# A two-layer perceiver block on one core: low halves on GpSimd, gated products in 512 columns

## The chip, the cores and the metric

The kernel runs on one core of one Trainium2 chip. A core has five engines with queues of their own: TensorE (PE) multiplies matrices into PSUM, VectorE (DVE), ScalarE (ACT) and GpSimd (POOL) do element-wise work, and SyncE (SP) here issues all the DMAs. GpSimd reads and writes only SBUF in this program; results in PSUM are read by DVE or ACT. The metric is the device time of one execution in microseconds (us), lower is better.

## The reference

There are 128 sequences of 32 tokens with 256 features, and a context of 257 tokens for each. Two layers follow each other, and each has three sublayers with a residual sum:

```python
x = x + L0_xattn(layernorm(x), ctx)      # A: 16 features a head, rms norm of q and k
x = x + L0_attn(layernorm(x))            # B: differential attention with rotary embedding
x = x + L0_ffn(layernorm(x))             # C: silu(x w1^T) * (x w2^T), 704 wide, weights rounded to NF4
x = x + L1_xattn(layernorm(x), mask, ctx) # D: 32 heads of 8; masked self-attention plus gated cross-attention
x = x + L1_attn(layernorm(x))            # E: 16 heads of 16, causal
x = x + L1_ffn(layernorm(x))             # F: router, 8 experts: w_e * ((silu(x Wg) * (x Wu)) Wd)
```

All inputs and outputs are float32.

## The kernel before

Four sequences make one block of 128 tokens, one token to a partition, so there are 32 blocks (`h`, or `u` where the context attention counts both layers). F and C take two blocks at a time (`g`, 16 of them).

**Precision.** A float32 operand of a matmul is split into a high and a low half of 16 bits, and a product is the sum of high x high, high x low and low x high. `split_ps` (lines 437 to 444) makes both halves from a PSUM bank: ACT copies the bank to float16 (high), and DVE subtracts that from the bank (low). `expP` (line 1026) does it in another way for the weights of the context attention: ACT writes the exponential as float32 (`P`), a bfloat16 view of its upper 16 bits serves as the high half, and POOL subtracts that view to make the low half (`Pl`). The hidden values of C and F (`hid`, `fhid`, with `hidl`, `fhl`) go that second way too.

**Streams and the order of work.** Each sublayer is a Python generator (`A_prep`, `rowpass`, `pvpass`, `attn_fin`, `B_gen`, `C_gen`, `D_prep`, `D_self`, `E_gen`, `E_att`, `F_gen`, `F_down`) that issues some instructions and yields. `pipeline` (line 411) holds a planner (`Est`): it has a cost for every instruction on each engine, keeps a time line of each engine, and always steps the stream whose next inputs are due first. The order it finds for each engine is pinned; the engines then wait for each other by semaphores. A change of any cost therefore rewrites the order of everything behind it. Every instruction is issued through line 290, so the profile's lines are all L290 and the names of the tiles tell the groups apart.

**PSUM** has 8 banks of 512 float32 columns. `tk` (line 386) hands out the one that the planner expects to be free first.

**The parts that the change touches:**
- `ln_raw` (533): two transposes of the block into a bank, the split into `hT`, and the statistics of the norm. B, D, E and A use it. `mm_tok` (495) multiplies `hT` by weights.
- `D_prep` (1273) makes queries, keys and values of a block for D; `D_self` (1325) does its self-attention: scores into `dS` (128 x 1024), a maximum over 32 columns for each of 32 groups (`s`), its subtraction, the exponential, then for each of two halves four transposes, the split into `dPT`, and the products with the values. The maximum is issued as follows:

```python
nc.vector.tensor_reduce(mx, Sf, AX.X, ALU.max)
nc.vector.tensor_tensor(Sf, Sf, mb, ALU.subtract)
nc.scalar.activation(Sf, Sf, AF.Exp)
```

- `E_gen` (1385) makes `qa`, `ka` and `va` of a block for E.
- `C_gen` (1231) and `F_gen` (1563): for each block of 128 hidden features, the gate and the up product of two token blocks (256 columns each) go side by side into one bank; ACT takes the tanh of the gate half (`glu_t`), DVE makes (tanh + 1) x gate and multiplies it by the up half, POOL makes the low half. C has six such blocks (the last of 64 features), F two for each of eight experts. `F_down` (1587) multiplies by the down weights, up to two experts behind.

The context work of layer 1 also prepares the keys and values that layer 2 reads back from DRAM.

Of the kernel before, what the change touches and what calls it, by code (L numbers as in the profile page):

```python
# [12 lines left out]
F32 = mybir.dt.float32  # L13
F16 = mybir.dt.float16
# [351 lines left out]
class Body:  # L366
# [70 lines left out]
    def split_ps(self, ps, hi, lo, scale=None):  # L437
# [4 lines left out]
        else:  # L442
            nc.scalar.activation(hi, ps, AF.Copy, scale=scale)
            nc.vector.scalar_tensor_tensor(lo, ps, scale, hi, ALU.mult, ALU.subtract)

    def rsqrt(self, o, a, eps):
        w, n = a.shape[0], a.shape[-1]
        if a.space != PSUM:
            self.nc.scalar.activation(o, a, AF.Copy, bias=eps)
        else:  # L450
            self.nc.vector.tensor_scalar(o, a, eps, None, ALU.add)
        self.nc.gpsimd.tensor_tensor(o, o, self.nhalf[:w, :n], ALU.pow)
# [42 lines left out]
    def mm_tok(self, ps, hT, tt, W, c0, N):  # L495
        nc = self.nc
        seq = [(a, b, k) for a, b in ((0, 0), (0, 1), (1, 0)) for k in (0, 1)]
        for i, (a, b, k) in enumerate(seq):
            nc.tensor.matmul(ps, hT[:, a, k, tt * 128:tt * 128 + 128], W[b][:, k, c0:c0 + N], start=(i == 0), stop=(i == len(seq) - 1))

# [6 lines left out]
    def ln_T(self, xts, pool, tag=None):  # L507
        nc = self.nc
        n = len(xts)
        mv = self.sm.tile([128, 2, 2], F32, name="bmv")  # L510
        for t in range(n):
            st = self.sm.tile([128, 6], F32, name="bst")
            nc.vector.bn_stats(st, xts[t])
            nc.vector.bn_aggr(mv[:, t, :], st)
        rs = self.sm.tile([128, 2], F32, name="brs")
        self.rsqrt(rs[:, :n], mv[:, :n, 1], 1e-5)
        hs = []
        nm = self.sm.tile([128, 2], F32, name="bnm")
        for t in range(n):
            nc.gpsimd.tensor_scalar(nm[:, t:t + 1], mv[:, t, 0:1], rs[:, t:t + 1], -1.0, ALU.mult, ALU.mult)  # L520
            h = pool.tile([128, 256], F32, name=f"lnh{t}", tag=tag, bufs=tag and n)
            nc.scalar.activation(h, xts[t], AF.Identity, bias=nm[:, t:t + 1], scale=rs[:, t:t + 1])
            hs.append(h)
        yield "end"
        ps = self.tk()
        for t, h in enumerate(hs):
            for k in range(2):
                nc.tensor.transpose(ps[:, (k * n + t) * 128:(k * n + t) * 128 + 128], h[:, k * 128:k * 128 + 128], self.ident)
        hT = pool.tile([128, 2, 2, 128 * n], F16, name="hT")
        self.split_ps(ps[:, :256 * n], hT[:, 0].rearrange("p k t -> p (k t)"), hT[:, 1].rearrange("p k t -> p (k t)"))  # L530
        return hT

    def ln_raw(self, xt, pool):
        nc = self.nc
        ps = self.tk()
        for k in range(2):
            nc.tensor.transpose(ps[:, k * 128:k * 128 + 128], xt[:, k * 128:k * 128 + 128], self.ident)
        hT = pool.tile([128, 2, 2, 128], F16, name="hT")
        self.split_ps(ps[:, :256], hT[:, 0].rearrange("p k t -> p (k t)"), hT[:, 1].rearrange("p k t -> p (k t)"))
# [616 lines left out]
    def setup_C(self):  # L1156
        nc, T = self.nc, self.T
        yield from self.need(("set", "A"))
        w1T = [self.w0.tile([128, 2, 704], BF, name=f"ffn{i}") for i in range(2)]
        self.w12T = w1T  # L1160
# [4 lines left out]
        for wi in range(3):  # L1165
# [47 lines left out]
            if wi < 2:  # L1213
                for k in range(2):
                    ps = self.tk().bitcast(BF)
                    for r in range(8):
                        nc.tensor.transpose(ps[:, r * 88:r * 88 + 88], wq[:, r * 256 + k * 128:r * 256 + k * 128 + 128], self.identb[:88, :88])
                    nc.vector.tensor_copy(w1T[wi][:, k, :].rearrange("p (s r) -> p r s", r=8), ps[:, :704].rearrange("p (r s) -> p r s", r=8))
                    yield "end"
            else:  # L1220
# [3 lines left out]
                for ft in range(6):  # L1224
# [4 lines left out]
                    yield "end"  # L1229

    def C_gen(self, g):
        nc = self.nc
# [5 lines left out]
        hl = self.cw.tile([128, 6, 256], F16, name="hidl")  # L1238
        for ft in range(6):
            n = FT[ft]  # L1240
            ps = self.tk()
            for u in range(2):
                seq = [(k, a) for k in (0, 1) for a in (0, 1)]
                for i, (k, a) in enumerate(seq):
                    nc.tensor.matmul(ps[:n, u * 256:u * 256 + 256], self.w12T[u][:, k, ft * 128:ft * 128 + n], hT[:, a, k, :], start=(i == 0), stop=(i == 3))
            t = self.cw.tile([128, 256], F32, name="glu_t", bufs=2)
            nc.scalar.activation(t[:n], ps[:n, :256], AF.Tanh, scale=0.5)
            nc.vector.scalar_tensor_tensor(t[:n], t[:n], 1.0, ps[:n, :256], ALU.add, ALU.mult)
            nc.vector.tensor_tensor(hid[:n, ft], t[:n], ps[:n, 256:512], ALU.mult)
            nc.gpsimd.tensor_tensor(hl[:n, ft], hid[:n, ft], hid[:n].bitcast(BF)[:, ft, 1::2], ALU.subtract)  # L1250
            yield "pe" if ft < 5 else [hl]
        hv = hid.bitcast(BF)
# [20 lines left out]
    def D_prep(self, h):  # L1273
# [6 lines left out]
        yield "end"  # L1280
        hT, rs = self.ln_raw(xt, self.dw)
        yield [hT, rs]
        yield from self.need(("cen",), *[("Ds", h - 1)] * (h > 0))
# [41 lines left out]
    def D_self(self, h):  # L1325
# [21 lines left out]
        nc.vector.tensor_reduce(mx, Sf, AX.X, ALU.max)  # L1347
        nc.vector.tensor_tensor(Sf, Sf, mb, ALU.subtract)
        nc.scalar.activation(Sf, Sf, AF.Exp)
# [3 lines left out]
        for q2 in range(2):  # L1353
            ps = self.tk()
            for q in range(4):
                nc.tensor.transpose(ps[:, q * 128:q * 128 + 128], S[:, q2 * 4 + q].rearrange("p b k -> p (b k)"), self.ident)
            PT = self.dw.tile([128, 2, 4, 128], F16, name="dPT")
            self.split_ps(ps, PT[:, 0].rearrange("p q t -> p (q t)"), PT[:, 1].rearrange("p q t -> p (q t)"))
            yield [PT]
            pr = self.tk()  # L1360
            for q in range(4):
                for a in range(2):
                    nc.tensor.matmul(pr[:, q * 4:q * 4 + 4], PT[:, a, q, :], self.ones4, start=(a == 0), stop=(a == 1))
            nc.vector.reciprocal(rs[:, :, q2 * 4:q2 * 4 + 4].rearrange("p b a -> p a b"), pr[:, :16].rearrange("p (a b) -> p a b", b=4))
            ps = self.tk()
            for q in range(4):
                qd = q2 * 4 + q
                for i, (a, d) in enumerate(((0, 0), (0, 1), (1, 0))):
                    nc.tensor.matmul(ps[:, q * 128:q * 128 + 128], PT[:, a, q, :], self.Vd[:, d, qd].rearrange("p b c -> p (b c)"), start=(i == 0), stop=(i == 2))
            for hh in range(4):  # L1370
# [14 lines left out]
    def E_gen(self, h):  # L1385
        nc = self.nc
        yield from self.need(("att", self.NH + h), ("set", "E"))
        xt = self.xt[self.NH + h]
        hT, rs = self.ln_raw(xt, self.ew)
        rq = self.sm.tile([128, 1], F32, name="rrq")  # L1390
        nc.scalar.activation(rq, rs, AF.Copy, scale=IWS)
        yield [hT, rq]
        ps = self.tk()
# [169 lines left out]
    def F_gen(self, g):  # L1563
# [6 lines left out]
        for e in range(8):  # L1570
            yield from self.need(*[("Fd", g * 8 + e - 2)] * (g * 8 + e > 1))
            hid = self.fw.tile([128, 2, 256], F32, name="fhid", bufs=2)
            hl = self.fw.tile([128, 2, 256], F16, name="fhl", bufs=2)
            for ft in range(2):
                ps = self.tk()
                for u, nm in enumerate((f"wg{e}", f"wu{e}")):
                    self.mm_feat(ps[:, u * 256:u * 256 + 256], self.W[nm], ft * 128, 128, lambda k: hT[:, 0, k, :], lambda k: hT[:, 1, k, :])
                t = self.fw.tile([128, 256], F32, name="glu_t", bufs=2)
                nc.scalar.activation(t, ps[:, :256], AF.Tanh, scale=0.5 * IWS)
                nc.vector.scalar_tensor_tensor(t, t, 1.0, ps[:, :256], ALU.add, ALU.mult)  # L1580
                nc.vector.tensor_tensor(hid[:, ft], t, ps[:, 256:512], ALU.mult)
                nc.gpsimd.tensor_tensor(hl[:, ft], hid[:, ft], hid.bitcast(BF)[:, ft, 1::2], ALU.subtract)
                yield "pe"
            self.fh[g * 8 + e] = (hid, hl, w)
# [192 lines left out]
```

## Time and profile before

| what | value |
|---|---|
| time, three runs | 3371.24, 3372.80, 3373.25 us; median 3372.8 |
| the profiled execution | 3372.91 us, of which the span of the instructions is 3371.1 |
| mean granted TensorE clock | 0.937 of full speed |
| context and layer 1, 300 to 1500 us: PE, DVE, ACT, POOL busy | 1153.2, 804.4, 956.3, 901.4 of 1200 us |
| passage between the layers, 1500 to 1800 us | 236.5, 207.1, 194.0, 159.3 of 300 us |
| layer 2, 1800 to 3300 us | 1361.5, 1182.7, 954.7, 914.0 of 1500 us |

The span is the time from the first to the last instruction of the program in one profiled execution. Busy time is the time in which an engine had an instruction at work; the end of a matmul is modelled, so a busy TensorE need not be TensorE at its peak. The granted clock is the share of the full clock that the throttle let TensorE have. In a row of groups, the shapes stand as out<-in (partitions x columns, type), then the count, the busy time, the mean of one instruction in ns, and the idle time of that engine just before those instructions with what ended it. "X <- Y" in a list of waits means that X stood idle until Y was done.

### The profile page before, as it was taken

The numbers are of one execution on the slowest core, as the hardware profiler recorded it, in microseconds if no ns is written. First come the engines' busy times: TensorE is split into PE (matmuls) and PEld (weight loads), VectorE is DVE, ScalarE is ACT, GpSimd is POOL, SyncE is SP. The second block draws the span as 40 slices with busy tenths as digits, with TensorE's granted clock in tenths as the row PEclk, the third lists the DMA queues.
The fourth block names the chain that finished last, engine by engine and source line by source line (L and its number), as shares of the span: only waits on it lengthen the run. The fifth ranks groups of instructions, "written<-read, shape, count | busy, mean of one in ns | idle before, by whom it ended". The sixth has DMA issues, their size and how long they took to land. (4 is left out here: it accounts for less than half of the span.)

```text
span 3371.1 us, 106946 instructions
## 1 busy us (share of the span) xinstructions
PE 3022.6 (90%) x41537; PEld 2271.9 (67%) x41537; DVE 2451.2 (73%) x6084; ACT 2246.3 (67%) x6477; POOL 2104.3 (62%) x2537
## 2 busy tenths in 40 slices
PE   3888999999999999998777999889989889989899
PEld 1455776666766666665555777667777777777677
DVE  4787666766667666666767778777888788787866
ACT  2455888878887787786666656666676666656562
POOL 1354787777777777775454756556666656656463
PEclk9899999999999999999876999889999899988889
DMA  4565777777777777776565444544454445445420
GB/s 105 156 178 156 207 220 213 223 214 209 217 222 215 220 204 206 211 219 168 142 163 135 111 107 98 126 111 113 110 133 100 121 106 123 107 98 122 107 60 14
DMA packets 687849, 511.64 MB, mean 152 GB/s; under 512 B 224396, under 2 KB 675340, under 8 KB 687340
## 3 DMA queue, kind: packets, MB, share of 16 engines
q1 hardware_dynamic: 687340, 504.80, 55.1%
q8 instruction: 326, 5.34, 0.7%
q14 instruction: 183, 1.50, 0.2%
HBM read 319.86 MB, written 180.19 MB: 148 GB/s over the span
## 5 line engine op out<-in xcount | busy, mean ns | idle before, releaser
L290 POOL TENSOR_TENSOR Pl<-P 128x512 f16<-128x512 f32 x768 | 805.9, 1064 | 241.3 <-ACT P L290 232.4
L290 DVE TENSOR_REDUCE mx<-bank 128x2 f32<-128x512 f32 x768 | 479.8, 679 | 28.2 <-PE bank L290 25.2
L290 ACT ACTIVATE P<-bank 128x512 f32<-128x512 f32 x768 | 438.6, 599 | 89.1 <-PE bank L290 63.1
L290 ACT COPY Uc<-bank 32x68 f32<-32x68 f32 x1536 | 314.7, 205 | 108.0 <-PE bank L290 88.3
L290 DVE TENSOR_TENSOR vv<-bank,vv 128x256 f16<-128x256 f32 x512 | 215.2, 424 | 145.2 <-ACT vv L290 139.7
L290 POOL TENSOR_TENSOR fhl<-fhid 128x256 f16<-128x256 f32 x256 | 156.5, 612 | 250.2 <-DVE fhid L290 238.8
L290 ACT CAST vv<-bank 128x256 f16<-128x256 f32 x512 | 203.3, 402 | 156.9 <-DVE vv L290 84.9
L290 PE MATMUL bank<-V,P 128*128 128x68 f16 (+1 forms) x4096 | 295.5, 197 | 10.4 <-DVE mx L290 3.9
L290 PE MATMUL bank<-V,Pl 128*128 128x36 f16 (+1 forms) x3072 | 280.8, 191 | 11.3 <-POOL Pl L290 9.3
L290 PEld LDWEIGHTS <-Kst 97*128 97x128 f16 x4096 | 232.8, 100 | 78.1 <-issue 51.2
L290 PEld LDWEIGHTS <-P 128*128 128x128 bf16 x4096 | 258.1, 100 | 24.5 <-issue 7.9
L290 ACT ACTIVATE glu_t<-bank 128x256 f32<-128x256 f32 x352 | 134.7, 383 | 192.3 <-PE bank L290 170.1
L290 PEld LDWEIGHTS <-Pl 128*128 128x128 f16 x3072 | 235.0, 98 | 37.0 <-POOL Pl L290 21.8
L290 DVE SCALAR_TENSOR_TENSOR glu_t<-glu_t,bank 128x256 f32<-128x256 f32 x352 | 145.1, 412 | 116.4 <-ACT glu_t L290 115.2
L290 PEld LDWEIGHTS <-ch 128*128 128x128 f16 x2048 | 191.7, 99 | 56.1 <-issue 27.2
L290 PE MATMUL bank<-QstD,Kst 97*128 97x128 f16 x2048 | 200.4, 228 | 27.8 <-DVE rbt L290 5.5
L290 PEld LDWEIGHTS <-hT 128*128 128x128 f16 x1536 | 138.5, 102 | 107.7 <-issue 30.5
L290 POOL TENSOR_TENSOR kk<-kb,kk 128x512 f16<-128x512 f32 x128 | 146.0, 1160 | 94.0 <-ACT kk L290 92.7
L290 PE MATMUL bank<-khf,eh 32*128 32x256 f16 (+1 forms) x1536 | 162.7, 284 | 46.4 <-DVE mx L290 10.2
L290 POOL TENSOR_TENSOR cl<-ct,ch 128x1024 f16<-128x1024 f32 x64 | 136.6, 2135 | 44.8 <-ACT ch L290 42.7
L290 DVE SCALAR_TENSOR_TENSOR xt<-bank,w,xt 128x256 f32<-128x256 f32 x256 | 120.0, 472 | 21.5 <-PE bank L290 20.1
L290 PEld LDWEIGHTS <-eh 32*128 32x128 f16 (+1 forms) x1536 | 53.1, 93 | 121.9 <-issue 107.9
(483 smaller groups left out, 9098.2 us busy)
## 6 DMA issues: line engine op xcount, KB each, us to landing
Kst<-kd SPq DMA_DIRECT2D x384, 256.0 KB
kd<-kk SPq DMA_DIRECT2D x128, 512.0 KB
vd<-vv SPq DMA_DIRECT2D x256, 136.0 KB
V<-vd SPq DMA_DIRECT2D x64, 544.0 KB
vd<-vv SPq DMA_DIRECT2D x256, 132.0 KB
V<-vd SPq DMA_DIRECT2D x64, 528.0 KB
ct<-in_ctxm SPq DMA_DIRECT2D x64, 512.0 KB
khf<-kd SPq DMA_DIRECT2D x128, 256.0 KB
```

Source lines behind the costliest of these rows:

```text
L290: r = f(*a, **k)
```

## The change

- `split_sb` is new. ACT copies the bank to float32 in SBUF; the upper 16 bits, read as bfloat16, are the high half, and POOL subtracts them from the copy to make the float16 low half. The blocks of D and E in `ln_raw` and the attention weights `dPT` of `D_self` use it in place of `split_ps`.
- In `D_self` the maxima are subtracted by POOL.
- C and F put two blocks of 128 hidden features into one step: two banks, one with two gate blocks and one with two up blocks, and tanh, products and low half over 512 columns (`glu`). C's weights are padded from 704 to 768 columns with zeros, so that its last block has 128 rows.
- In `E_gen` one ACT instruction with a repeated operand writes both copies of the keys' high half.
- Tiles grow to fit: `lnh` shares the tag of `glu_t` and so is allotted 512 columns. The program's dynamic DMA scratch is set to 8192.

```diff
+    def split_sb(self, ps, pool, name, tag=None, **kw):
+        nc = self.nc
+        n = ps.shape[-1]
+        f = pool.tile([128, n], F32, name=name, tag=tag, **kw)
+        nc.scalar.copy(f, ps)
+        hi = f.bitcast(BF)[:, 1::2]
+        lo = pool.tile([128, n], F16, name=name + "l", tag=tag and tag + "l", **kw)
+        nc.gpsimd.tensor_tensor(lo, f, hi, ALU.subtract)
+        return hi, lo
...
-    def ln_raw(self, xt, pool):
+    def ln_raw(self, xt, pool, pooled=False):
...
-        hT = pool.tile([128, 2, 2, 128], F16, name="hT")
-        self.split_ps(ps[:, :256], ...)
+        if pooled:
+            hT = tuple(x.rearrange("p (k t) -> p k t", k=2) for x in self.split_sb(ps[:, :256], pool, "hT", "hT"))
+        else:
+            hT = pool.tile([128, 2, 2, 128], F16, name="hT")
+            self.split_ps(ps[:, :256], ...)
...
+    def glu(self, t, ps, out, sc):
+        nc = self.nc
+        nc.scalar.activation(t, ps[0], AF.Tanh, scale=sc)
+        nc.vector.scalar_tensor_tensor(t, t, 1.0, ps[0], ALU.add, ALU.mult)
+        nc.vector.tensor_tensor(out, t, ps[1], ALU.mult)
...
     def C_gen(self, g):
-        for ft in range(6):
-            n = FT[ft]
-            ps = self.tk()
+        for f2 in range(3):
+            f = slice(2 * f2, 2 * f2 + 2)
+            ps = [self.tk() for _ in range(2)]
             for u in range(2):
...
-            t = self.cw.tile([128, 256], F32, name="glu_t", bufs=2)
-            nc.scalar.activation(t[:n], ps[:n, :256], AF.Tanh, scale=0.5)
-            nc.vector.scalar_tensor_tensor(t[:n], t[:n], 1.0, ps[:n, :256], ALU.add, ALU.mult)
-            nc.vector.tensor_tensor(hid[:n, ft], t[:n], ps[:n, 256:512], ALU.mult)
-            nc.gpsimd.tensor_tensor(hl[:n, ft], hid[:n, ft], hid[:n].bitcast(BF)[:, ft, 1::2], ALU.subtract)
-            yield "pe" if ft < 5 else [hl]
+            t = self.cw.tile([128, 512], F32, name="glu_t", bufs=2)
+            self.glu(t, ps, hid[:, f].rearrange("p f t -> p (f t)"), 0.5)
+            nc.gpsimd.tensor_tensor(hl[:, f], hid[:, f], hid.bitcast(BF)[:, f, 1::2], ALU.subtract)
+            yield "pe" if f2 < 2 else [hl]
...
     def D_prep(self, h):
-        hT, rs = self.ln_raw(xt, self.dw)
-        yield [hT, rs]
+        hT, rs = self.ln_raw(xt, self.dw, True)
+        yield [hT[1], rs]
...
     def D_self(self, h):
-        nc.vector.tensor_tensor(Sf, Sf, mb, ALU.subtract)
+        nc.gpsimd.tensor_tensor(Sf, Sf, mb, ALU.subtract)
...
-            PT = self.dw.tile([128, 2, 4, 128], F16, name="dPT")
-            self.split_ps(ps, PT[:, 0].rearrange("p q t -> p (q t)"), PT[:, 1].rearrange("p q t -> p (q t)"))
-            yield [PT]
+            PT = [x.rearrange("p (q t) -> p q t", q=4) for x in self.split_sb(ps, self.dw, "dPT", "dPT")]
+            yield [PT[1]]
...
     def E_gen(self, h):
-        hT, rs = self.ln_raw(xt, self.ew)
+        hT, rs = self.ln_raw(xt, self.ew, True)
...
+        p2 = pk.unsqueeze(2).to_broadcast([128, 16, 2, 16])
+        nc.scalar.activation(kb[0], p2, AF.Copy, scale=rq)
         for i in range(2):
-            nc.scalar.activation(kb[0][:, :, i, :], pk, AF.Copy, scale=rq)
             nc.vector.scalar_tensor_tensor(kb[1][:, :, i, :], pk, rq, kb[0][:, :, i, :], ALU.mult, ALU.subtract)
...
     def F_gen(self, g):
-            for ft in range(2):
-                ps = self.tk()
-                for u, nm in enumerate((f"wg{e}", f"wu{e}")):
-                    self.mm_feat(ps[:, u * 256:u * 256 + 256], ...)
-                t = self.fw.tile([128, 256], F32, name="glu_t", bufs=2)
...
-                yield "pe"
+            ps = [self.tk() for _ in range(2)]
+            for u, nm in enumerate((f"wg{e}", f"wu{e}")):
+                for ft in range(2):
+                    self.mm_feat(ps[u][:, ft * 256:ft * 256 + 256], ...)
+            t = self.fw.tile([128, 512], F32, name="glu_t", bufs=2)
+            self.glu(t, ps, hid.rearrange("p f t -> p (f t)"), 0.5 * IWS)
+            nc.gpsimd.tensor_tensor(hl, hid, hid.bitcast(BF)[:, :, 1::2], ALU.subtract)
+            yield "pe"
...
-    nc = bacc.Bacc("TRN2", target_bir_lowering=False, num_devices=1)
+    nc = bacc.Bacc("TRN2", target_bir_lowering=False, num_devices=1, dynamic_dma_scratch_size=8192)
```

More of the change, by code (lines that the diff above doesn't have):

```diff
@@ L498, in mm_tok @@
         for i, (a, b, k) in enumerate(seq):
-            nc.tensor.matmul(ps, hT[:, a, k, tt * 128:tt * 128 + 128], W[b][:, k, c0:c0 + N], start=(i == 0), stop=(i == len(seq) - 1))
+            x = hT[a][:, k] if isinstance(hT, tuple) else hT[:, a, k]
+            nc.tensor.matmul(ps, x[:, tt * 128:tt * 128 + 128], W[b][:, k, c0:c0 + N], start=(i == 0), stop=(i == len(seq) - 1))
     def mm_feat(self, ps, W, c0, M, xh, xl):
@@ L520, in ln_T @@
             nc.gpsimd.tensor_scalar(nm[:, t:t + 1], mv[:, t, 0:1], rs[:, t:t + 1], -1.0, ALU.mult, ALU.mult)
-            h = pool.tile([128, 256], F32, name=f"lnh{t}", tag=tag, bufs=tag and n)
+            h = pool.tile([128, 512], F32, name=f"lnh{t}", tag=tag, bufs=tag and n)[:, :256]
             nc.scalar.activation(h, xts[t], AF.Identity, bias=nm[:, t:t + 1], scale=rs[:, t:t + 1])
@@ L537, in ln_raw @@
             nc.tensor.transpose(ps[:, k * 128:k * 128 + 128], xt[:, k * 128:k * 128 + 128], self.ident)
-        hT = pool.tile([128, 2, 2, 128], F16, name="hT")
-        self.split_ps(ps[:, :256], hT[:, 0].rearrange("p k t -> p (k t)"), hT[:, 1].rearrange("p k t -> p (k t)"))
+        if pooled:
+            hT = tuple(x.rearrange("p (k t) -> p k t", k=2) for x in self.split_sb(ps[:, :256], pool, "hT", "hT"))
+        else:
+            hT = pool.tile([128, 2, 2, 128], F16, name="hT")
+            self.split_ps(ps[:, :256], hT[:, 0].rearrange("p k t -> p (k t)"), hT[:, 1].rearrange("p k t -> p (k t)"))
         mv = self.sm.tile([128, 2], F32, name="rmv")
@@ L1158, in setup_C @@
         yield from self.need(("set", "A"))
-        w1T = [self.w0.tile([128, 2, 704], BF, name=f"ffn{i}") for i in range(2)]
+        w1T = [self.w0.tile([128, 2, 768], BF, name=f"ffn{i}") for i in range(2)]
+        for t in w1T:
+            nc.vector.memset(t[:, :, 704:], 0.0)
         self.w12T = w1T
@@ L1217, in setup_C @@
                         nc.tensor.transpose(ps[:, r * 88:r * 88 + 88], wq[:, r * 256 + k * 128:r * 256 + k * 128 + 128], self.identb[:88, :88])
-                    nc.vector.tensor_copy(w1T[wi][:, k, :].rearrange("p (s r) -> p r s", r=8), ps[:, :704].rearrange("p (r s) -> p r s", r=8))
+                    nc.vector.tensor_copy(w1T[wi][:, k, :704].rearrange("p (s r) -> p r s", r=8), ps[:, :704].rearrange("p (r s) -> p r s", r=8))
                     yield "end"
@@ L1238, in C_gen @@
         hl = self.cw.tile([128, 6, 256], F16, name="hidl")
-        for ft in range(6):
-            n = FT[ft]
-            ps = self.tk()
+        for f2 in range(3):
+            f = slice(2 * f2, 2 * f2 + 2)
+            ps = [self.tk() for _ in range(2)]
             for u in range(2):
-                seq = [(k, a) for k in (0, 1) for a in (0, 1)]
-                for i, (k, a) in enumerate(seq):
-                    nc.tensor.matmul(ps[:n, u * 256:u * 256 + 256], self.w12T[u][:, k, ft * 128:ft * 128 + n], hT[:, a, k, :], start=(i == 0), stop=(i == 3))
-            t = self.cw.tile([128, 256], F32, name="glu_t", bufs=2)
-            nc.scalar.activation(t[:n], ps[:n, :256], AF.Tanh, scale=0.5)
-            nc.vector.scalar_tensor_tensor(t[:n], t[:n], 1.0, ps[:n, :256], ALU.add, ALU.mult)
-            nc.vector.tensor_tensor(hid[:n, ft], t[:n], ps[:n, 256:512], ALU.mult)
-            nc.gpsimd.tensor_tensor(hl[:n, ft], hid[:n, ft], hid[:n].bitcast(BF)[:, ft, 1::2], ALU.subtract)
-            yield "pe" if ft < 5 else [hl]
+                for ft in range(2):
+                    seq = [(k, a) for k in (0, 1) for a in (0, 1)]
+                    for i, (k, a) in enumerate(seq):
+                        nc.tensor.matmul(ps[u][:, ft * 256:ft * 256 + 256], self.w12T[u][:, k, (2 * f2 + ft) * 128:(2 * f2 + ft) * 128 + 128], hT[:, a, k, :], start=(i == 0), stop=(i == 3))
+            t = self.cw.tile([128, 512], F32, name="glu_t", bufs=2)
+            self.glu(t, ps, hid[:, f].rearrange("p f t -> p (f t)"), 0.5)
+            nc.gpsimd.tensor_tensor(hl[:, f], hid[:, f], hid.bitcast(BF)[:, f, 1::2], ALU.subtract)
+            yield "pe" if f2 < 2 else [hl]
         hv = hid.bitcast(BF)
@@ L1362, in D_self @@
                 for a in range(2):
-                    nc.tensor.matmul(pr[:, q * 4:q * 4 + 4], PT[:, a, q, :], self.ones4, start=(a == 0), stop=(a == 1))
+                    nc.tensor.matmul(pr[:, q * 4:q * 4 + 4], PT[a][:, q, :], self.ones4, start=(a == 0), stop=(a == 1))
             nc.vector.reciprocal(rs[:, :, q2 * 4:q2 * 4 + 4].rearrange("p b a -> p a b"), pr[:, :16].rearrange("p (a b) -> p a b", b=4))
@@ L1368, in D_self @@
                 for i, (a, d) in enumerate(((0, 0), (0, 1), (1, 0))):
-                    nc.tensor.matmul(ps[:, q * 128:q * 128 + 128], PT[:, a, q, :], self.Vd[:, d, qd].rearrange("p b c -> p (b c)"), start=(i == 0), stop=(i == 2))
+                    nc.tensor.matmul(ps[:, q * 128:q * 128 + 128], PT[a][:, q, :], self.Vd[:, d, qd].rearrange("p b c -> p (b c)"), start=(i == 0), stop=(i == 2))
             for hh in range(4):
@@ L1388, in E_gen @@
         xt = self.xt[self.NH + h]
-        hT, rs = self.ln_raw(xt, self.ew)
+        hT, rs = self.ln_raw(xt, self.ew, True)
         rq = self.sm.tile([128, 1], F32, name="rrq")
         nc.scalar.activation(rq, rs, AF.Copy, scale=IWS)
-        yield [hT, rq]
+        yield [hT[1], rq]
         ps = self.tk()
@@ L1573, in F_gen @@
             hl = self.fw.tile([128, 2, 256], F16, name="fhl", bufs=2)
-            for ft in range(2):
-                ps = self.tk()
-                for u, nm in enumerate((f"wg{e}", f"wu{e}")):
-                    self.mm_feat(ps[:, u * 256:u * 256 + 256], self.W[nm], ft * 128, 128, lambda k: hT[:, 0, k, :], lambda k: hT[:, 1, k, :])
-                t = self.fw.tile([128, 256], F32, name="glu_t", bufs=2)
[L1579 to L1582, printed above, removed]
-                yield "pe"
+            ps = [self.tk() for _ in range(2)]
+            for u, nm in enumerate((f"wg{e}", f"wu{e}")):
+                for ft in range(2):
+                    self.mm_feat(ps[u][:, ft * 256:ft * 256 + 256], self.W[nm], ft * 128, 128, lambda k: hT[:, 0, k, :], lambda k: hT[:, 1, k, :])
+            t = self.fw.tile([128, 512], F32, name="glu_t", bufs=2)
+            self.glu(t, ps, hid.rearrange("p f t -> p (f t)"), 0.5 * IWS)
+            nc.gpsimd.tensor_tensor(hl, hid, hid.bitcast(BF)[:, :, 1::2], ALU.subtract)
+            yield "pe"
             self.fh[g * 8 + e] = (hid, hl, w)
```

## The prediction

> **What bounds the kernel now.** I read first the busy times on the page, then a table by stretch, then who ends TensorE's idle time, then single instructions in order of time.
>
> ```profile
> PE 3022.6 (90%) x41537; PEld 2271.9 (67%) x41537; DVE 2451.2 (73%) x6084; ACT 2246.3 (67%) x6477; POOL 2104.3 (62%) x2537
> ```
>
> TensorE is the fullest engine, but that share is a mean. The table by stretch separates layer 1 with its context work (300 to 1500 us), the passage between the layers, and layer 2 (1800 to 3300 us); its columns are the stretch, its length, busy us and instructions of PE, weight loads, DVE, ACT, POOL, then the granted clock, the DMA share and GB/s. Two 100-us slices of layer 2 follow.
>
> ```profile
> 300.00:1500.00 1200.00, 1153.17 (x12935) 830.44 (x12935) 804.44 (x2057) 956.27 (x2702) 901.38 (x1053) 0.99 0.73 214
> 1800.00:3300.00 1500.00, 1361.49 (x23162) 1094.50 (x23161) 1182.68 (x2939) 954.71 (x2857) 914.00 (x1147) 0.92 0.45 108
> ```
>
> ```profile
> 2000.00:2100.00 100.00, 95.26 (x1645) 77.51 (x1645) 82.53 (x207) 65.63 (x200) 62.94 (x82) 0.97 0.50 117
> 2100.00:2200.00 100.00, 85.99 (x1381) 67.44 (x1378) 74.44 (x193) 62.79 (x187) 58.55 (x73) 0.86 0.46 109
> ```
>
> Layer 1 is TensorE's own: 96% busy at a clock of 0.99. Layer 2 has 138.5 us of idle TensorE in 1500, a clock of 0.92, and DVE as the fullest helper at 78.8% (1182.68 / 1500), ahead of ACT at 63.6% and POOL at 60.9%. A slice in which TensorE stalls also has the lower clock and fewer matmuls. So what the change is worth is decided in layer 2. The waits of TensorE there (total us, times, longest):
>
> ```profile
> PE bank L290 <- DVE mx L290: 15.7, 56, 1.6
> PE bank L290 <- DVE hT L290: 15.4, 16, 2.7
> PE bank L290 <- ACT P L290: 15.2, 35, 1.2
> PE bank L290 <- DVE fhid L290: 14.2, 14, 2.6
> ...
> PE bank L290 <- POOL Pl L290: 4.5, 10, 0.7
> ```
>
> Summed by the engine that ended them, with the smaller rows: DVE 75.5 us, ACT 36.0, POOL 9.3. The weight loads, which run ahead of the matmuls, were held 23.5 us by POOL. Why DVE is late is seen in the order of time (start, duration, engine, line, operation); rows of other engines are left out:
>
> ```profile
> 2404.41 1.21 DVE L290 TENSOR_REDUCE s<-dS 128x32 f32<-128x1024 f32 x1
> ...
> 2404.94 0.39 ACT L290 ACTIVATE glu_t<-bank 128x256 f32<-128x256 f32 x1 [0.45 <-PE bank L290]
> ...
> 2405.65 1.28 DVE L290 TENSOR_TENSOR dS<-dS,s 128x1024 f32<-128x1024 f32 x1
> ...
> 2406.85 0.41 DVE L290 SCALAR_TENSOR_TENSOR glu_t<-glu_t,bank 128x256 f32<-128x256 f32 x1
> ```
>
> The tanh is ready at 2405.33, but the product that needs it starts at 2406.85, behind the maximum and its subtraction in D_self. The bank stays taken for those 1.5 us. That is a queue on DVE, and the change takes the subtraction out of it.
>
> **The change, part by part.** Prices come from these groups (busy us, mean ns, then idle before them):
>
> ```profile
> L290 POOL TENSOR_TENSOR Pl<-P 128x512 f16<-128x512 f32 x768 | 805.9, 1064 | 241.3 <-ACT P L290 232.4 <-DMA mk<-in_mask 5.7 <-ACT pl L290 1.6
> L290 DVE TENSOR_TENSOR fhid<-glu_t,bank 128x256 f32<-128x256 f32 x256 | 107.3, 419 | 11.9 <-DVE glu_t L290 0.5
> L290 DVE TENSOR_TENSOR hT<-bank,hT 128x256 f16<-128x256 f32 x128 | 53.2, 417 | 40.7 <-ACT hT L290 38.2 <-DMA Kst<-kd 1.3 <-DMA wst<-in_wg 0.4
> L290 DVE TENSOR_TENSOR dPT<-bank,dPT 128x512 f16<-128x512 f32 x64 | 43.7, 682 | 13.6 <-ACT dPT L290 13.3
> L290 DVE TENSOR_TENSOR dS<-dS,s 128x1024 f32<-128x1024 f32 x32 | 42.4, 1326 | 0.5
> L290 POOL TENSOR_TENSOR eS<-eS,emx 128x512 f32<-128x512 f32 x32 | 33.5, 1047 | 81.5 <-DVE emx L290 41.6 <-ACT ue L290 12.8 <-DVE s L290 8.5
> ```
>
> *Low halves.* D_prep and E_gen lose 64 DVE subtractions of 417 ns (26.7 us) and D_self 64 of 682 ns (43.7). POOL gets 64 of 256 columns at 612 ns (the row of fhl: 39.2 us) and 64 of 512 at 1064 (68.1). ACT's copy costs the same into float32 as into float16 (aTE copy 588 ns, dPT cast 587), and the weight loads from a strided bfloat16 view cost what the float16 ones do (P 101 ns, Pl 98).
>
> *Maxima.* DVE loses 42.4 us. POOL gets 32 subtractions of 1024 columns with a broadcast operand, an operation that is not in the trace. The nearest rows are 629 ns for 256 columns (ue) and 1047 for 512 (eS), 1.63 ns a column, so 1047 + 512 x 1.63 = 1883 ns, or 60.3 us. Below, it can't be under 1.05; above, twice 1047 is 2.09, so 33 to 67 us.
>
> *Gated products.* In F, DVE has 256 x (412 + 419) ns = 212.7 us. At 512 columns each operation costs about 685 ns (dPT 682, eS from a bank 690): 128 x 1.37 = 175.4, so -37.3. POOL goes from 256 x 612 (156.7) to 128 x 1064 (136.2), -20.5. The tanh goes from 256 x 383 (98.0) to 128 x 599 (the exponential P, same shape: 76.7), -21.3. E_gen's two key copies of 470 ns become one of about 0.69 (470 + 256 x 0.84, the step from 383 to 599): -8 on ACT. C, in layer 1, saves about 14 us of DVE, 8 of ACT and 8 of POOL. It lies under a TensorE at 96% and 0.99, with 46.8 us idle in 1200: worth 0 to 5, I take 0. Its last block, now 128 columns of weights, moves the same 256 columns; a wider load is not a longer wait there.
>
> *Two banks per expert.* A gate bank and an up bank instead of two mixed ones. With matmuls of 107 ns, one mixed bank is held for 12 x 0.107 + 0.383 + 0.412 + 0.419 = 2.5 us, two for 5.0. After, the tanh starts when the gate bank is full, while the up matmuls run: gate 1.28 + 0.60 + 0.685 = 2.6, up from 1.28 until 3.28 = 2.0, in sum 4.6. So it is no more bank time. The chain after the last matmul grows from 1.8 to about 1.8 to 2.4 us, under cover of F_down's two-expert lag. If that cover fails, the waits on fhid (14.2 us) double; if the banks come free sooner, they vanish: +14 to -14, taken as 0 since both sums are near.
>
> *DMA scratch, padding.* All DMAs are issued by SP on the hardware queue, so the halved scratch has nothing to slow that the trace shows; the two memsets are in set-up. Both 0.
>
> Sum in layer 2: DVE -26.7 - 43.7 - 42.4 - 37.3 = -150 us; POOL +39.2 + 68.1 + 60.3 - 20.5 = +147; ACT -29; TensorE 0. DVE goes from 78.8% to 68.8%, POOL from 60.9% to 70.7%, ACT to 61.7%.
>
> *What that is worth.* I let the waits on an engine go as its share over its idle share. DVE: 0.788/0.212 = 3.72 to 0.688/0.312 = 2.21, a factor 0.60. POOL: 1.56 to 2.41, x1.55. ACT: x0.92. Of DVE's 75.5 us, four fifths of the hT row (64 of its 80 instructions in layer 2 move; 12.3 us) go to POOL. There is the new wait: TensorE's first projections of D and E wait for POOL, which may be inside an instruction of 1.06 or 1.88 us, and everything behind them on TensorE's queue waits too.
> - DVE: 63.2 x 0.60 = 37.9, so -25.3
> - hT, now on POOL: 12.3 x 1.5 = 18.5, so +6.2
> - POOL's own: 9.3 x 1.55 = 14.4, so +5.1
> - ACT: 36.0 x 0.92, so -2.9
> - weight loads behind POOL: 23.5 x 1.55 would be +13; they run ahead, so 0 here, 13 in the range
>
> Stalls: -16.9 us. The clock comes on top: 0.08 x 1500 = 120 us of pulses are withheld beside 138.5 us of idle time, 0.87 us for each, so -14.7. Together -31.6. The profiled execution took 3372.9 us (span 3371.1), the median of the runs is 3372.8: 3341.
>
> The Trainium skill, "TensorE: Matmul & The Clock Gate" (Part 1), has the clock halved only after an idle window of about 3.4 us. The longest waits above are 2.7 us and the clock is 0.92 all the same, so here shorter stalls go with the loss; by the page alone the clock's 14.7 us would drop out and the time be 3356. The page "GPSIMD Engine Reference" (4.1, Engine selection) speaks against the change: two-input elementwise work belongs to VectorE, GpSimd being about twice as slow. The rows give 1064 / 682 = 1.56; at twice, POOL would get 58 us more (74.6% busy), and the same sum would end some 15 us later.
>
> **The rivals.** *POOL takes DVE's place* (slower). For it: POOL serves its queue in order, pv needs each Pl, and 1.9-us blocks now stand among them. If POOL ended as much idle time as DVE does now on TensorE and its loads (75.5 + 19.0 = 94.5 against 9.3 + 23.5 + 12.3 = 45.1), that is +49, less 25 and 3, +21 of stalls, x1.87 with the clock +40: 3413. It decides once POOL's part grows by over 28 us, a factor 1.6. Against it: POOL idles 576 us in the stretch, and at 71% would still be under DVE's present share. *Nothing moves*: the planner's new order stalls elsewhere; DVE, ACT and bank waits are many small ones. Between -6.7 and +6.7, 3373. *The clock follows fully*: the four slices at 0.97 carry 1645, 1599, 1632 and 1639 matmuls per 100 us; 23162 at their mean of 1629 take 1422 us, so -78: 3295. For it: DVE's bursts are gone; against it: those slices have the fullest DVE too.
>
> **How the numbers follow.** 0.50 for the forecast (-10 to -55), 0.18 for the full clock, 0.12 for nothing, 0.20 for POOL. 0.2% (6.7 us) is about what a measurement of this kernel can tell. Faster 0.68, same 0.12, slower 0.20. The range reaches half into both outer cases: 3290 to 3392.
>
> **What would show it.** In the same stretch: DVE near 69% and POOL near 71%; TensorE's idle time ended by DVE near 38 us, by POOL about 33; a clock of 0.93 to 0.94; the POOL subtraction near 1.9 us; layer 1 unchanged. It is wrong if POOL ends more idle time than DVE, if the clock falls, or if the passage at 1500 to 1800 us grows.

## The result, and the profile after

The changed kernel took 3390.9 us (median of six runs, 3387.4 to 3398.6), before took 3372.0 (six runs, 3364.2 to 3376.9): a ratio of 1.006, 95% interval 1.0041 to 1.0079. The forecast was 3341 and faster. The time is inside the range, on the other side of no change.

First the busy times on the page of after, then the same two stretches as before.

```profile
PE 3031.7 (90%) x41537; PEld 2288.9 (68%) x41537; DVE 2296.2 (68%) x5574; ACT 2223.9 (66%) x6269; POOL 2219.9 (66%) x2521
```

```profile
300.00:1500.00 1200.00, 1157.99 (x13089) 836.81 (x13088) 804.72 (x1997) 965.61 (x2689) 909.78 (x1028) 0.99 0.74 217
1800.00:3300.00 1500.00, 1345.12 (x22923) 1085.75 (x22909) 1038.58 (x2526) 926.29 (x2683) 1006.15 (x1156) 0.90 0.45 108
```

The work went where it was meant to: in layer 2 DVE fell from 1182.7 to 1038.6 us of 1500 (69.2%) and POOL rose from 914.0 to 1006.2 (67.1%). Layer 1 kept its clock and its busy share, and came through a little sooner: matmul 14500 of 41537 ends at 1486.7 us, in before at 1500.6. The end of the span is 15.7 us later, so about 30 us were lost behind layer 1. There, in the stretch of layer 2, TensorE began fewer matmuls (22923 instead of 23162) and the clock fell from 0.92 to 0.90. The new instructions cost what their rows had promised; busy us, then mean ns:

```profile
L290 POOL TENSOR_TENSOR dPTl<-dPT 128x512 f16<-128x512 f32 x64 | 66.7, 1042 | 46.8 <-ACT dPT L290 46.6
L290 POOL TENSOR_TENSOR dS<-dS,s 128x1024 f32<-128x1024 f32 x32 | 61.2, 1914 | 1.7 <-DVE s L290 1.6
L290 POOL TENSOR_TENSOR hTl<-hT 128x256 f16<-128x256 f32 x64 | 39.6, 621 | 38.9 <-ACT hT L290 38.2 <-PE bank L290 0.5
L290 DVE TENSOR_TENSOR fhid<-glu_t,bank 128x512 f32<-128x512 f32 x128 | 87.7, 685 | 14.9 <-PE bank L290 1.7 <-DVE glu_t L290 0.5
```

The waits of TensorE in layer 2 of after (total us, times, longest):

```profile
PE bank L290 <- DMA QstD<-ed: 21.8, 6, 5.1
PE bank L290 <- ACT hT L290: 19.5, 10, 5.8
PE bank L290 <- issue: 17.3, 11, 4.5
PE bank L290 <- DVE mx L290: 15.9, 35, 3.4
...
PE bank L290 <- DVE glu_t L290: 7.9, 12, 1.2
PE bank L290 <- POOL Tm L290: 7.4, 4, 2.5
PE bank L290 <- POOL Pl L290: 4.6, 11, 0.8
```

Summed by the engine that ended them, as in the prediction: DVE 75.5 to 41.6 us, ACT 36.0 to 47.7, POOL 9.3 to 18.6, DMA 1.9 to 23.8, issue 9.3 to 17.3. DVE gave back 34 us, and others took 51. Two of the new names belong to D's preparation. The first is the chain that ends with QstD (start, duration, what):

```profile
2856.82 1.29 ACT el L290 x3
...
2859.15 6.24 DMA ed<-el
...
2865.41 2.91 DMA QstD<-ed
...
2868.37 0.66 PE bank L290 x11
```

TensorE stood 3.79 us before that last row. The second is the wait for hT, and its longest case shows what ACT was waiting for; the brackets hold the idle time before the instruction and what ended it:

```profile
2543.71 0.37 ACT L290 COPY hT<-bank 128x256 f32<-128x256 f32 x1 [5.79 <-DMA Vd<-vs]
...
2544.13 0.61 PE L290 MATMUL bank<-khf,eh 32*128 32x256 f16 x4 [5.79 <-ACT hT L290]
```

The values `vs` share a buffer with `hT`. ACT's copy into it can start only when the DMA into Vd, which reads `vs`, is through; everything behind it on ACT's queue waits too, and so does TensorE. Before has the same wait, one engine further along:

```profile
2128.14 0.37 ACT L290 CAST hT<-bank 128x256 f16<-128x256 f32 x1 [2.82 <-DMA Vd<-vs]
...
2128.54 0.42 DVE L290 TENSOR_TENSOR hT<-bank,hT 128x256 f16<-128x256 f32 x1 [2.01 <-ACT hT L290]
...
2129.02 1.18 PE L290 MATMUL bank<-khf,eh 32*128 32x256 f16 x4 [1.60 <-DVE hT L290]
```

### The profile page after: what moved, and what is told of

It reads as the page before. It is cut to its first block, busy times and chain, and to the rows that moved or that the text cites. A ratio compares the mean times of both kernels' runs of the same rounds, so it can differ in the third digit from the quotient of the medians.

```text
span 3386.8 us, 106219 instructions
## 1 busy us (share of the span) xinstructions
PE 3031.7 (90%) x41537; PEld 2288.9 (68%) x41537; DVE 2296.2 (68%) x5574; ACT 2223.9 (66%) x6269; POOL 2219.9 (66%) x2521
## 4 chain that ended last, share of the span: by engine, by line
PE 56%; DVE 14%; DMA 11%; ACT 9%; issue 5%; POOL 4%; SPq 2%; DVEq 0%; ACTq 0%; POOLq 0%
PE bank L290 56%; DVE mx L290 3%; SPq L290 2%; ACT P L290 1%; DVE vv L290 1%; ACT vv L290 1%; ACT Uc L290 1%; POOL Pl L290 1%; DVE nfmk L290 1%; DMA QstA<-mT 1%; DMA kd<-kk 1%; DMA Vd<-vs 1%; DMA QstD<-ed 1%; DMA ed<-el 1%; DVE kb L290 1%
## 5 line engine op out<-in xcount | busy, mean ns | idle before, releaser
L290 POOL TENSOR_TENSOR Pl<-P 128x512 f16<-128x512 f32 x768 | 789.6, 1045 | 151.9 <-ACT P L290 149.7
L290 PE MATMUL bank<-V,P 128*128 128x68 f16 (+1 forms) x4096 | 305.3, 198 | 9.5 <-ACT P L290 4.0
L290 PE MATMUL bank<-V,Pl 128*128 128x36 f16 (+1 forms) x3072 | 288.9, 194 | 11.3 <-POOL Pl L290 9.7
L290 POOL TENSOR_TENSOR fhl<-fhid 128x512 f16<-128x512 f32 x128 | 133.3, 1041 | 213.0 <-DVE fhid L290 207.3
L290 PEld LDWEIGHTS <-Pl 128*128 128x128 f16 x3072 | 242.4, 99 | 39.8 <-POOL Pl L290 21.8
L290 PE MATMUL bank<-QstD,Kst 97*128 97x128 f16 x2048 | 205.6, 234 | 15.7 <-DVE mx L290 4.9
L290 DVE SCALAR_TENSOR_TENSOR glu_t<-glu_t,bank 128x512 f32<-128x512 f32 x176 | 119.9, 681 | 101.8 <-ACT glu_t L290 100.9
L290 ACT ACTIVATE glu_t<-bank 128x512 f32<-128x512 f32 x176 | 105.2, 598 | 95.8 <-PE bank L290 90.9
L290 PEld LDWEIGHTS <-hT 128*128 128x128 f16 (+1 forms) x1280 | 111.2, 101 | 71.3 <-issue 16.2
L290 DVE SCALAR_TENSOR_TENSOR xt<-bank,xt 128x256 f32<-128x256 f32 x160 | 66.5, 418 | 123.0 <-PE bank L290 116.7
```

The source lines that it names most:

```text
L290: r = f(*a, **k)
```

## The experiments

The theories: (1) D's chain of copies and DMAs became late; (2) any rewritten order shifts the time as much as the change did; (3) the coarser products carry the loss; (4) the change costs time in the mean over orders. Later ones are named in the expectations. The planner pins an order that depends on every cost and latency it assumes, so an order can be changed with no instruction touched. Before, in this section, is 3372.0; each run was also timed beside before on its own chip, and ratios are against that.

**One part at a time.** `low_only`, `max_only` and `glu_only` are before with one of the three parts; the key copy of E_gen is in none of them, and all three have the DMA scratch of 8192.

```diff
 low_only:  split_sb in D_prep, E_gen and dPT; everything else as before
 max_only:
-        nc.vector.tensor_tensor(Sf, Sf, mb, ALU.subtract)
+        nc.gpsimd.tensor_tensor(Sf, Sf, mb, ALU.subtract)
 glu_only:  two banks and 512 columns in C and F; everything else as before
```

> Before, with only the low halves of the D and E blocks and of dPT made by POOL (maxima, products and the key copy as before). Theory 1 (the new waits come from D's chain of copies and DMAs, which begins with the low halves now made by POOL): this part carries the loss, 10 to 20 us slower than before, with waits of TensorE on the landing of QstD. Theory 2 (any rewritten order of the planner shifts the time by as much as the change did): anywhere within 15 us of before. Theory 3 (the coarser products carry the loss): 5 to 15 us faster, since DVE loses 70 us.

> Before, with only the maxima of D_self subtracted by POOL. Theory 1: no loss, 0 to 10 us faster, since DVE loses 42 us and POOL gains 61 at a place that is not in the DMA chain. Theory 2: anywhere within 15 us. Theory 3: 0 to 10 us faster.

> Before, with only the gated products of C and F in 512 columns (and C's padded weights). Theory 1: 0 to 10 us faster, no new waits on DMAs. Theory 2: anywhere within 15 us. Theory 3 (a step of 24 matmuls and two banks is harder to place, and the instructions behind it on DVE and POOL wait longer): 10 to 25 us slower.

Measured: the low halves 3405.4 (ratio 1.0095, 1.0077 to 1.0113), the maxima 3379.0 (1.0011, 0.9996 to 1.0026), the products 3401.7 (1.0092, 1.0065 to 1.0118). Two parts alone were each slower than all of them together, so the parts do not add, and none of the theories was told apart by this.

**The same instructions in another order.** One constant of the planner moves by 2 ns.

```diff
-    LAT = {"pe": 196.0, "act": 150.0, "dve": 135.0, "pool": 75.0, "dma": 910.0}
+    LAT = {"pe": 196.0, "act": 152.0, "dve": 135.0, "pool": 75.0, "dma": 910.0}   # j1
+    LAT = {"pe": 196.0, "act": 148.0, "dve": 135.0, "pool": 75.0, "dma": 910.0}   # j2
+    LAT = {"pe": 196.0, "act": 150.0, "dve": 137.0, "pool": 75.0, "dma": 910.0}   # j3
```

> Before, with the same instructions; the planner only takes ACT's results to be visible after 152 ns instead of 150, so that it finds another order. Theory 1 and theory 3: within 5 us of before. Theory 2: 5 to 20 us away from before, in either direction.

> Before with the same instructions in another order: the planner takes ACT's results to be visible after 148 ns instead of 150. If orders scatter by as much as the parts of the change did (theory 2), this lies 5 to 30 us from before; if orders scatter by no more than the other perturbed order did (8 us), within 10 us.

> After with the same instructions in another order (ACT's results visible after 152 ns). Theory 2: 5 to 30 us from after, and as likely as not under the time of before. If the change itself costs time whatever the order (theory 4): within 10 us of after, 3380 to 3400.

> After in a third order (ACT's results visible after 148 ns). Theory 2: 5 to 30 us from after, no matter of which sign; theory 4: 3380 to 3400.

> Before in a fourth order (the planner takes DVE's results to be visible after 137 ns instead of 135). Three orders of before took 3366, 3373 and 3398: again in 3355 to 3400.

> After in a fourth order (DVE's results visible after 137 ns). Three orders of after took 3391, 3412 and 3430. If the change costs time in the mean over orders (theory 4): 3390 to 3430. If the three were chance (theory 2): 3355 to 3400.

| order | before, us | after, us |
|---|---|---|
| as it was | 3372.0 | 3390.9 |
| j1 | 3365.6 | 3430.4 |
| j2 | 3397.6 | 3412.4 |
| j3 | 3385.7 | 3415.6 |
| mean, standard deviation | 3380.3, 14.3 | 3412.3, 16.3 |

An order alone is worth up to 32 us (3365.6 to 3397.6 with the same instructions). That is theory 2, and it would explain the measured 19 us. But the means differ by 32.1 us, with a standard error of 10.8 (both deviations, four orders each), and after is slower in each of the four pairs: theory 4 holds as well, though j1 and j2 of after lie above the 3380 to 3400 that it had set for them (j1 is 39.5 us from after, outside theory 2's 30 too). The change itself costs about 32 us, and its own order was its luckiest of four.

**The shared buffer.**

```diff
-        vs = self.dw.tile([128, 2, 256], F16, name="vs", tag="hT")
+        vs = self.dw.tile([128, 2, 256], F16, name="vs")
```

> After, with a buffer of its own for the values vs of D, which share one with the block's high half hT there. Theory 1 (D's chain of copies and DMAs is what became late): ACT no longer stands 20 us before hT for the landing of Vd, TensorE's 20.7 us behind hT on ACT shrink to under 8, and the time falls by 10 to 25 us. Theory 2: ACT's wait goes, the time moves by up to 30 us in either direction with the new order.

> Before, with a buffer of its own for D's vs. In before, TensorE's 18.6 us behind hT on DVE may be this same wait under another name, since DVE's low half waits for ACT's copy, and that for the landing of Vd. Theory 5 (the shared buffer costs both kernels the same, and the change only renames the wait): 10 to 25 us faster than before, under 3365. Theory 2 (only the order counts): within 30 us of before in either direction; ACT's 15 us before hT go in both.

> After with the buffer of its own, in another order (ACT's results visible after 152 ns; without the buffer that order took 3430). Theory 1 and 5 (the buffer is worth 20 to 30 us in any order): 3400 or less, at least 25 us under 3430. Theory 2: anywhere from 3360 to 3430.

Measured: 3360.7 instead of 3390.9 in after (ratio to before 0.9977, 0.9958 to 0.9996), 3392.0 instead of 3430.4 in its order j1 (1.0053, 1.0035 to 1.0071), and 3349.4 instead of 3372.0 in before (0.9913, 0.9884 to 0.9943). So 23 to 38 us in three of three. Each is one order against one, and the buffer's name changes the order too, so a single difference can be off by some 20 us (the scatter of two orders); three of the same sign are harder to put down to that. ACT's row of waits for Vd, which in after reads

```profile
ACT hT L290 <- DMA Vd<-vs: 23.2, 9, 5.8
```

is gone from all three. TensorE's wait behind hT on ACT in layer 2 fell from 19.5 to 1.6 us in after, and behind hT on DVE from 15.4 to 4.0 in before. Theory 5 is borne out: both kernels paid for the buffer. Theory 1 is half right, since the wait is real but not new. In before most of it stood under DVE's name (`DVE hT`: DVE's low half waits for ACT's copy, and that for Vd); in after DVE no longer makes that half, and the same wait stands under ACT's. Before with the buffer of its own is the fastest kernel of the study and beats both.

**More orders of two parts.** The edits are those above, put together.

> The low halves alone, in a second order (ACT's results visible after 152 ns). Four orders of before had a mean of 3380. Theory 6 (the low halves on POOL cost time in any order: D's and E's projections now hang on one more engine): 3395 to 3425. Theory 2 (the first order was a bad one): as likely under 3390 as over it.

> The low halves alone, in a third order (DVE's results visible after 137 ns). Theory 6: 3395 to 3425; theory 2: as likely under 3390 as over it.

> The gated products of 512 columns alone, in a second order (ACT's results visible after 152 ns). Theory 7 (POOL's 1.04-us low half stands before Pl at the wrong time: TensorE and its loads wait for POOL 37 and 64 us, where the orders of before have 11 and 27, although POOL has less to do): POOL's waits again over 25 and 45 us, time 3390 to 3420. Theory 2: the waits and the time return to those of before.

> The gated products of 512 columns alone, in a third order (DVE's results visible after 137 ns). Theory 7: POOL's waits over 25 and 45 us, time 3390 to 3420; theory 2: as before.

Measured: the low halves 3372.9 (1.0004, 0.9986 to 1.0023) and 3406.5 (1.0114, 1.0093 to 1.0136), with the first order a mean of 3394.9: 15 us above the mean of before, with a standard error of 13, which is unsettled. The products 3426.1 (1.0170, 1.0145 to 1.0195) and 3417.2 (1.0148, 1.0128 to 1.0168), with the first order a mean of 3415.0: 35 us above before, with a standard error of 10. The wide products carry the loss. The maxima were timed in one order alone and lie inside the scatter of before.

Theory 7 was only half met. TensorE and its loads waited for POOL 30 and 51 us in j1, over its bounds of 25 and 45, but 21 and 40 in j3, under them; the mean of before's four orders is 11 and 27. The time of j1 is over the 3420 of the theory. And Pl starts no later behind P: 1.0 to 1.1 us in the three orders of the products, 1.1 to 1.3 in the four of before (from the trace, after 1650 us). So a Pl that is held up in POOL's queue does not explain the waits.

**The step, or the instructions behind it.** In F the products alone run 24 matmuls without a break; before ran 12. In the traces after 1650 us before has 215 unbroken runs of 12 gate and up matmuls, median 1.5 us, the products alone 112 of 24, median 2.8. One run cuts the step, the other the instructions: the first has 219 runs of 12 again, the second 114 of 24.

```diff
 glu_yield, in F:
+            ps = [self.tk(True)]
...
+            for u, nm in enumerate((f"wg{e}", f"wu{e}")):
+                if u:
+                    yield "pe"
+                    ps.append(self.tk())
...
+                if not u:
+                    nc.scalar.activation(t, ps[0], AF.Tanh, scale=0.5 * IWS)
...
 glu_256, in F:
+            for ft in range(2):
+                c = slice(ft * 256, ft * 256 + 256)
+                self.glu(t[:, c], [x[:, c] for x in ps], hid[:, ft], 0.5 * IWS)
+                nc.gpsimd.tensor_tensor(hl[:, ft], hid[:, ft], hid.bitcast(BF)[:, ft, 1::2], ALU.subtract)
```

> The wide products alone, but in F the step of 24 matmuls is cut into two steps of 12 (gate, then up), with the gate's bank held in between; tanh, products and low half stay at 512 columns. The wide products alone took 3402, 3426 and 3417. Theory 8 (the long step on TensorE is what costs: nothing else can be placed between its matmuls): 3360 to 3395, and the half-clock time after 1650 us falls from about 403 to under 370 us. Theory 9 (the wider instructions on ACT, DVE and POOL cost): 3400 to 3430 as before.

> The wide products alone, but in F tanh, products and low half are cut into two of 256 columns each, behind the same step of 24 matmuls into two banks. Theory 8: 3400 to 3430, the loss remains. Theory 9: 3365 to 3395, the loss goes, and TensorE's waits for POOL return from 29 us to 11.

Measured: with the step cut, 3371.5 (1.0003, 0.9981 to 1.0025); with the instructions cut, 3427.5 (1.0168, 1.0143 to 1.0194). Layer 2 of the first and then of the second:

```profile
1800.00:3300.00 1500.00, 1352.99 (x23071) 1086.04 (x23072) 1143.21 (x2690) 932.63 (x2718) 893.87 (x1022) 0.92 0.45 108
```

```profile
1800.00:3300.00 1500.00, 1326.27 (x22419) 1067.68 (x22418) 1138.81 (x2847) 921.81 (x2743) 876.82 (x1093) 0.90 0.45 107
```

With steps of 12 the 512-column instructions are level with before, and the clock is back at 0.92. With 256-column instructions behind a step of 24 the whole loss is there, with 652 fewer matmuls in the stretch and the clock at 0.90. Theory 8 holds, with its half-clock time too (338 us, under 370); theory 9 falls, and the waits for POOL that it expected at 11 us are 37. Each is one order, and the difference of two single orders scatters by some 20 us (14 times the root of two), so the 56 us between them are about 2.8 times that. All kernels with the old buffer say the same: the eight with steps of 24 took 3391 to 3430 us, mean 3415; the nine with steps of 12 took 3366 to 3407, mean 3384. Their waits of TensorE in layer 2, the cut step first:

```profile
PE bank L290 <- DVE mx L290: 20.7, 53, 3.4
PE bank L290 <- DVE hT L290: 16.7, 15, 4.3
PE bank L290 <- DVE xt L290: 14.7, 13, 4.2
PE bank L290 <- ACT P L290: 13.8, 28, 1.0
```

```profile
PE bank L290 <- DVE mx L290: 21.2, 38, 6.9
PE bank L290 <- DVE glu_t L290: 16.9, 16, 3.1
PE bank L290 <- ACT P L290: 15.4, 20, 2.0
```

No single wait makes the difference. After 1650 us TensorE's stalls (idle times of over 0.15 us) sum to 183 us with the cut step and 223 us with the cut instructions; of the 41 between them POOL ends 18 and DMAs 14. The clock was at half for 338 and 425 us, of which TensorE was busy in 289 and 341: about 26 us of pulses lost to work. In the mean, before has 184 us of stalls and 288 us busy at half clock, the three orders of the products alone 198 and 341: 14 us of stalls and 26 of pulses, beside a loss of 35.

The cut of the step does two more things: the gate's tanh is issued before the up matmuls, and the up bank is taken half a step later. A wait for the two banks of a long step is not what costs. In front of F's own gate and up matmuls TensorE stalled 12.6 us in the mean of before, 8.9 with the products, 12.7 with the cut step and 3.3 with the cut instructions. What grew are the stalls in front of other streams: before the products of V with P and Pl they are 14, 31, 22 and 35 us in the same order. A likely reading is that the experts' matmuls are what fills TensorE while other chains run, and that half as many pieces of double size fill fewer gaps. These counts fit it; the share of the earlier tanh was not timed by itself.

## Why the prediction was wrong, point by point

**What bounds the kernel** was read rightly as to place: the loss lies behind layer 1. In the mean of four orders each, matmul 14500 ends 4 us sooner in after, inside the 0 to 5 us that C was given, matmul 18000 ends at 1841 us in both, and the span ends at 3407 instead of 3380. In the two orders that were compared first, 11 of the 30 us went between these two matmuls, in the passage, and 19 behind them.

**The sums of work** held. DVE fell by 155 us over the span against 164 (150 in layer 2 and 14 in C), POOL rose by 116 against 139, partly because Pl fell from 1064 to 1045 ns, ACT fell by 22 against 37. The unseen POOL subtraction took 1914 ns for the 1883 taken. Three small figures of the working are off without weight: the gate and up matmuls start 109 ns apart, not 107, dPT's cast took 588 ns, not 587, and 2.21 / 3.72 is 0.59. The Trainium skill, "GPSIMD Engine Reference" (4.1, Engine selection), has GpSimd about twice as slow as VectorE for two-input elementwise work; the runs show 1042 / 682 = 1.53, close to the 1.56 that the sum had used.

**DVE's waits** fell as forecast in size, to 41.6 us where 37.9 was left for DVE, but not for the stated reason alone. The hT row was taken for a queue on DVE. Most of it is a wait for a buffer that a DMA still reads, so it did not move to POOL for 18.5 us but to ACT for 19.5. The low halves alone show how little a lighter DVE queue was worth: DVE lost 66 us of work there after 1650 us (durations summed, 1491 to 1426 in the means), and the waits of TensorE on it went from 98 to 89. Nor did TensorE gain from the relief as a whole. Its idle time in layer 2 was to fall by 16.9 us and rose by 16.4 (138.5 to 154.9). In the means over orders, after (3412) is level with the products alone (3415), so the low halves and maxima, with about 113 us less work for DVE, gained nothing clear of an error of 11 us. Why the relief brought nothing beyond the waits named here is open.

**"Two banks per expert", priced at 0, is the step that failed.** The bank time was counted, and may well be no more than before. TensorE stalled no more before F's own gate and up matmuls than it had (8.9 us for 12.6). What was not counted is that the step also sets how finely TensorE's work can be cut: 24 matmuls instead of 12. The products cost 35 us in three orders where the term stood at 0, and the last pair puts that down to the step, with 3427 against 3371. This is about half of the way from the forecast 31.6 us faster to the 32 slower of the means; the rest is the gain that did not come.

**Waits for POOL** were 9.3 to 18.6 us for the 14.4 forecast, and the loads' wait behind POOL 23.5 to 42.1: +19, where 13 was the upper end. On TensorE alone POOL ended less idle time than DVE (18.6 to 41.6), but with the weight loads, as the rival counted, more (60.7 to 54.8). The rival that POOL takes DVE's place still did not come to pass: it needed 28 us more behind POOL, and there were 16 (60.7 for 45.1). That the mean of after's orders, 3412, is the rival's 3413 is chance.

**DMA and issue** were not in the sum. The 20 us more behind QstD look like a cost of the change, but before's own order was lucky there: after 1650 us its four orders wait 17 us for DMAs in the mean, after's 24.

**The clock** was forecast to rise to 0.93 or 0.94 and fell to 0.90, which the prediction had named as a sign of being wrong. It had priced 0.87 us of pulses for each us of idle time, and that proportion does not hold: the products alone have 8% more stalls than before (198 / 184) and 20% more half-clock time (403 / 337). The Trainium skill, "TensorE: Matmul & The Clock Gate" (Part 1), halves the clock after an idle window of about 3.4 us; after 1650 us before has two stalls of TensorE over 3.4 us (4.5 and 3.6, neither among the prediction's lines) and 47 stretches of half clock, so a stall of that length is not needed. The traces show what is. The clock in them is full or half and nothing else, and the changes to half after 1650 us lie, in each trace, on a grid of 3.41 us. Over the 20 traces, a window of that grid at full clock in which TensorE was busy for less than half the time was followed by half clock in 410 of 421 cases, one busy for 70 to 80% in 103 of 504, and one over 90% in 50 of 5717. The way back is harder: at half clock, none of the 460 windows under 70% busy was the last of its stretch, and 762 of the 932 at 99% or more were. So in these traces short stalls go with half clock where they fall close together or into a stretch already at half clock, and a total of idle time cannot price them; it takes how evenly TensorE is fed, which the order of the instructions changes.

**"Nothing moves"** was given 6.7 us to either side. Orders of the same instructions scatter by 14 to 16 us, so that case should have been wider than most effects in the sum, with the range of the likeliest case to match. That 3390.9 lies inside the range at all is the luck of its order: the other three took 3412 to 3430.

## What to carry to other kernels

Where a planner interleaves streams, the size of a step is a cost of its own: in this kernel wider instructions on the helpers were cheap, longer unbroken runs on the bound engine were not, and the two can be cut apart. Before pricing a wait by the load of the engine that ended it, look at what that engine was waiting for, since a DMA that still reads a shared buffer can stand under any of their names. And time a few meaningless orders first: here they scatter by 15 us, so one run of each part says little about parts worth 20.

## What the runs showed of the hardware

Taking 155 us of work off the helper with the most waits shortened nothing by itself. The granted clock of TensorE in layer 2 was 0.90, 0.93 and 0.90 for the same instructions in three orders (the low halves alone, 3405, 3373 and 3407 us). It fell to half after a window of 3.41 us in which TensorE was busy for less than half the time (410 of 421), and came back only after one with few gaps. POOL's subtraction took 621, 1042 and 1914 ns for 256, 512 and 1024 columns, where DVE's had taken 417, 682 (both from a PSUM bank) and 1326. A buffer shared across a DMA (Vd, 3.48 us at 2853 us of after) cost 23 to 38 us in kernels of 3372 to 3430.
